# Graph attention and graph convolution on one core: four score tiles in a row from shared PSUM, and both ends reordered

## The chip, the core and the metric

The kernel runs on one core of one Trainium2 chip. A core has a tensor engine (PE, with its weight loads shown as PEld), VectorE (DVE), ScalarE (ACT), GpSimd (POOL) and SyncE (SP), which here only starts DMAs. Each engine works through its own instructions in order. The time is the device time of one execution in microseconds (us); a kernel's time is the median of its runs.

## The reference

There are 32 batches of 512 nodes with 512 features, all in float32, and one adjacency matrix of 512 x 512 for all of them.

```python
# layer 0: attention with 8 heads of 64, masked by the adjacency matrix
q, k, v = x @ Wq + bq, x @ Wk + bk, x @ Wv + bv
weights = softmax(q k^T / 8 + where(adj == 0, -1e9, 0))
x = layernorm(x + weights v)
# layer 1: graph convolution with a normalised adjacency matrix
deg = adj.sum(axis=1)
norm_adj = adj * rsqrt(deg)[:, None] * rsqrt(deg)[None, :]
x = layernorm(x + norm_adj @ (x @ W1) + b1)
```

## The kernel before

**Products.** The products with Wv, Wk, Wq and W1 are made of 512 x 512 matrices cut in two both ways, with seven products of halves instead of eight (`seven`, `second`). Each such *piece* is eight matmuls into one PSUM bank named `mm`, and VectorE or ScalarE adds it to what it belongs to. The seven products need sums and differences of the operands: slots 4, 5, 6 and a changed slot 2 of `XT` (x transposed, made by `combine`), of `wv`, `wk`, `wq`, `w1` (made by `weigh_part`), and of `zT` (made by the `combine` in `convolve`).

**Attention.** A *block* is one batch and one pair of heads, so there are 4 blocks to a batch and 128 in all; the loop over k goes through them. For a block, `scores` makes four score tiles of 128 x 1024 (two heads beside each other), in two calls with two tiles each. Each tile is four matmuls of 64 rows into two PSUM banks. VectorE cuts the tile off at 60 and subtracts the mask (`e<-sc,maskT`), which frees the PSUM, and ScalarE takes the exponent in place. `values` multiplies the tiles by v into one bank, `av`, with 64 columns for each head; VectorE turns that into `yb`, and DMAs bring it to its place in `YT`. GpSimd adds up the tiles for the softmax's sums (`accumulate`, some of it put off through `pending`), and VectorE folds the sums (`fold`, a transpose and a reduction).

**Order.** Every engine's order is the order in which the program is written (`InOrder` pins it). Step k of the loop runs the first two score tiles of block k, folds the sums of block k - 1, runs the values of block k - 1, then the last two score tiles of block k, then a *share* of other work: the values, keys and queries of the next batch and the convolution of the batch before, which is 8 pieces to a block. The lists `main`, `side` and `beside` say which small step follows which piece, and `cut` makes the shares. In the first batch a share has 4 pieces. The convolution's steps are `norm` (layer norm and its float32r part `hi`), `low` (the remainder `lo`), `lift` (adds b1), `grow` (scales by the root of the degree), `first` or `block` (times the adjacency), `second` (times W1), `measure`, `root` and `store`.

**PSUM.** There are eight banks. Three are for pieces and small things (`ps_mm`), two times two for score tiles (`ps_sc`), and one for `av` (`ps_av`).

**Ends.** Ahead of the loop stand the loading and weighing of the weights (`weigh(wv)`, `weigh(wk)` on GpSimd), `turn_first` (x of batch 0 turned by PE), the values and keys of batch 0 and the masks (`adjacency`). `compare` checks that the float32r adjacency lost nothing, and `degrees` makes the powers of the degrees. Behind the loop stands what is left of the last two batches, and `judge` and a count, from which the program decides on the device whether its shortcuts held; if they did not, `general` computes everything again.

Of the kernel before, what the change touches and what calls it, by code (L numbers as in the profile page):

```python
# [9 lines left out]
F32 = mybir.dt.float32  # L10
# [7 lines left out]
P = 128  # L18
H = 8
# [30 lines left out]
def unshifted(  # L50
# [29 lines left out]
    B, N, D = x.shape  # L80
# [9 lines left out]
    small = ctx.enter_context(tc.tile_pool(name="small", bufs=3))  # L90
    ps_mm = ctx.enter_context(tc.tile_pool(name="ps_mm", bufs=3, space=bass.MemoryType.PSUM))
    ps_sc = ctx.enter_context(tc.tile_pool(name="ps_sc", bufs=2, space=bass.MemoryType.PSUM))
    ps_av = ctx.enter_context(tc.tile_pool(name="ps_av", bufs=1, space=bass.MemoryType.PSUM))

# [23 lines left out]
    def turn(b, j):  # L118
# [4 lines left out]
        if j == 0 and b > 1:  # L123
            load_x(b, 1)

    def turn_first(j, i):

        p = ps_mm.tile([P, 2, HALF], F32, name="mm")
        for n in range(2):
            for u in range(2):  # L130
                for q in range(4):
                    at = q * P + (2 * i + u) * 32
                    tensor.matmul(
                        p[32 * q : 32 * (q + 1), u, ts(n, P)], R[0][2 * j + n][:, at : at + 32], ident,
                        start=True, stop=True,
                    )
        (scalar.copy if i else vector.tensor_copy)(XT[:, 2 * j + i], p)

# [102 lines left out]
    def adjacency(m):  # L241


        p = ps_mm.tile([P, N], F32, name="mm")
# [41 lines left out]
    def seven(multiply, first, middle, out):  # L286
# [3 lines left out]
        def piece(k, i, j):  # L290
            p = ps_mm.tile([P, 2, HALF], F32, name="mm")
            multiply(p, i, j)
# [22 lines left out]
    def values_of(b):  # L315


        def multiply(p, i, j):
            for r in range(2):
                for u in range(2):  # L320
                    tensor.matmul(
                        p[:, r, :], XT[:, j, u, ts(r, P)], wv[:, i, u, :],
                        start=u == 0, stop=u == 1,
                    )

        def first(e1, p):
# [46 lines left out]
    def scores(s):  # L373
# [3 lines left out]
        for l in range(2):  # L377
            j = 2 * jj + l
            e = E[s][l]
            p = ps_sc.tile([P, 2, N], F32, name="sc")  # L380
            for k in range(2):
# [26 lines left out]
    def values(s):  # L408
# [3 lines left out]
        if jj == 0:  # L412
            AV[b, g] = ps_av.tile([P, N], F32, name="av")
        av = AV[b, g]
# [45 lines left out]
    def sums(b, c):  # L460


        p = ps_mm.tile([P, N], F32, name="mm")
        for q in range(4):
# [33 lines left out]
    def finish(b):  # L498
# [4 lines left out]
        def inverse_all():  # L503

            p = ps_mm.tile([P, H, NT, 4], F32, name="mm")
            tensor.matmul(
# [11 lines left out]
        def inverse(cs):  # L518
            sT = SM[b]
            p = ps_mm.tile([P, NT, 2, 2, 32], F32, name="mm")  # L520
            for i in range(NT):
# [25 lines left out]
        def turn_values(g):  # L547

            t["y"] = ps_mm.tile([P, NT, P], F32, name="mm")
            for i in range(NT):  # L550
# [46 lines left out]
        def lift(i):  # L597
            gpsimd.tensor_add(YT[b][:, i, :], YT[b][:, i, :], b1_r)

# [31 lines left out]
    def convolve(b):  # L631
# [5 lines left out]
        def first(d):  # L637
            p = ps_mm.tile([P, N], F32, name="mm")
            for m in range(NT):
# [4 lines left out]
        def block(m):  # L644
            if m == 0:
                t["p"] = [ps_sc.tile([P, 2, N], F32, name="sc") for _ in range(2)]
            for part, start, stop in ((HI[b][:, m, :], m == 0, False), (LO[b][m], False, m == NT - 1)):
# [27 lines left out]
        def second(k, i, j):  # L675
            p = ps_mm.tile([P, 2, HALF], F32, name="mm")
            for r in range(2):
# [123 lines left out]
    weigh(wv, gpsimd)  # L801
    weigh(wk, gpsimd)
    first = values_of(0)
# [20 lines left out]
    run(one)  # L824
    shares, rest, within = [], [], []
    for k in range(S + 1):
        b, at = divmod(k, G)
        if at == 1:
# [10 lines left out]
            if b == 0:  # L839
# [3 lines left out]
                beside = {  # L843
                    2: put_off, 3: [(0, degrees, ())] + put_off, 6: put_off, 7: w1_parts[:1] + put_off,
                    8: w1_parts[1:2], 9: turn0 + w1_parts[2:3], 10: put_off + exact[:2], 11: put_off + w1_parts[3:],
                    12: exact[2:], 13: turn1,
                }
                side = early[5:6] + put_off + early[6:] + put_off
                side += sum(([piece] + beside.get(i, []) for i, piece in enumerate(main)), [])
                shares = cut(side, (4, 4, 4, 4))  # L850
            elif b < B - 1:
# [4 lines left out]
                beside = {  # L856
                    0: rest[:1], 1: rest[1:3], 3: rest[3:4] + put_off, 4: rest[4:5],
                    5: rest[5:6] + f["inverse"] + put_off, 6: rest[6:] + f["scale"][:2], 7: f["scale"][2:] + f["add"],
                    8: measure[:2] + put_off, 9: measure[2:], 10: f["root"] + put_off, 11: norm[:1],
                    12: norm[1:2] + low[:1], 13: norm[2:3] + low[1:2], 14: norm[3:] + low[2:3],  # L860
                    15: low[3:] + f["lift"], 16: put_off + grow[:2], 17: put_off + grow[2:], 18: turn0 + f["judge"],
                }
                side = sum(([piece] + beside.get(i, []) for i, piece in enumerate(main)), [])
                side += c["first"] + c["parts"] + kq[5:] + turn1[:1]
                s = c["second"]
                if b < B - 2:
                    side += put_off + s[:1] + put_off + s[1:3] + turn1[1:2] + s[3:4] + turn1[2:3] + s[4:5]
                    side += turn1[3:4] + s[5:6] + c["measure"][:1] + turn1[4:] + s[6:] + c["measure"][1:2]
                    rest = c["measure"][2:] + c["root"] + c["store"]
                    shares = cut(side, (8, 8, 8, 8))  # L870
# [22 lines left out]
        if k < S:  # L893
            scores((*blocks[k], 0))
        if k == 0:
            run(two)
            early = values_of(1)
            run(early[:2])
        if k and blocks[k - 1][0] < B - 1:
            fold(*blocks[k - 1])  # L900
        if k:
            values((*blocks[k - 1], 0))
# [3 lines left out]
            if k == S - 2:  # L906
                sums(blocks[k - 1][0], (k - 1) % G // 2)
        if k == S - 2:
# [12 lines left out]
        if k == 0:  # L921
            run(early[2:3] + put_off + early[3:4] + put_off + early[4:5])
        elif shares:
            run(shares.pop(0))
# [4 lines left out]
    run(sum((pairs[3][i : i + 1] + end["measure"][i : i + 1] for i in (0, 1)), []) + end["halves"][:1] + s[3:5])  # L929
    run(sum((pairs[3][i : i + 1] + end["measure"][i : i + 1] for i in (2, 3)), []) + extend[:1] + end["halves"][1:])  # L930
# [15 lines left out]

    run(e["unload"] + e["parts"] + s[6:] + end["grow"] + extend[2:] + c["measure"][:2])
    s, tail, halves = e["second"], c["measure"][2:] + c["root"] + c["store"], e["halves"]
    run(s[:2] + halves[0] + s[2:3] + tail[:1] + s[3:4] + tail[1:3] + s[4:5])
    p = ps_mm.tile([1, 1], F32, name="mm")  # L950
    tensor.matmul(p, count, ones, start=True, stop=True)
    vector.tensor_scalar(bad, p, -1.0, float(P * B * NT * H + N), op0=ALU.mult, op1=ALU.add)
    run(tail[3:] + s[6:] + e["measure"][2:] + e["roots"][1:] + e["stores"][2:] + s[5:6] + halves[1] + e["roots"][:1])
    run(e["stores"][:2])
# [283 lines left out]
```

## Time and profile before

| what | us |
|---|---|
| median of three runs | 2820.21 (2820.18 to 2822.76) |
| the profiled execution, its own time | 2821.64 |
| its span, first to last instruction | 2819.7 |
| PE busy | 2792.0 |
| VectorE busy | 2177.5 |
| GpSimd busy | 1786.4 |
| ScalarE busy | 1050.1 |

The span is one profiled execution. An engine is busy while one of its instructions runs, and matmuls overlap their neighbours, so a busy PE can still lose time between matmuls of different shapes. Every instruction that goes through `InOrder` is recorded with line 44, so rows are told apart by the names of what they write and read: `sc<-kq` are scores, `av<-e,v` are values, `mm<-...` are pieces. A row `a, b <- c` ends with what the engine waited for before it. A stretch's row gives its length, the busy time of PE, PEld, DVE, ACT and POOL with the number of instructions, the granted PE clock, the DMA engines' share and GB/s. The granted clock was 0.997 over the span.

### The profile page before, as it was taken

How to read it: one execution, taken by the hardware profiler on the slowest of the kernel's cores; microseconds unless marked ns; L12 is line 12 of the kernel's file. 1: busy time of each engine (PE TensorE's matmuls, PEld its weight loads, DVE VectorE, ACT ScalarE, POOL GpSimd, SP SyncE). 2: the span in 40 equal slices, each digit the busy share in tenths (PEclk: the TensorE clock that was granted, in tenths of full speed). 3: DMA queues.
4: the chain of work that ended last, by engine and by line, in shares of the span. 5: the costliest groups of instructions: out<-in, count | busy, mean ns of one | idle time of the engine just before them, and what ended most of it. 6: DMA issues, size and time to landing. Idle time of an engine off the chain costs nothing.

```text
span 2819.7 us, 34592 instructions
## 1 busy us (share of the span) xinstructions
PE 2792.0 (99%) x12540; PEld 1874.8 (66%) x12540; DVE 2177.5 (77%) x3201; ACT 1050.1 (37%) x1323; POOL 1786.4 (63%) x1174
## 2 busy tenths in 40 slices
PE   8999999999999999999999999999999999999997
PEld 6566666666666666666666666666666666666655
DVE  5877877788777787777787778877777777778777
ACT  2333333343333433334333334333343333443343
POOL 3666665666666666666666666666666666666656
PEclk9999999999999999999999999999999999999999
DMA  4111121112221122221112211222112122112211
GB/s 120 32 29 49 49 59 43 43 48 52 57 57 42 38 52 54 57 45 42 49 49 60 53 42 37 53 56 57 42 41 53 49 56 46 42 49 49 60 38 50
DMA packets 379107, 141.04 MB, mean 50 GB/s; under 512 B 277808, under 2 KB 345392, under 8 KB 378928
## 3 DMA queue, kind: packets, MB, share of 16 engines
q1 hardware_dynamic: 377776, 137.17, 20.4%
q8 instruction: 101, 1.65, 0.2%
q10 hardware_dynamic: 1152, 1.57, 0.2%
q14 instruction: 78, 0.64, 0.1%
HBM read 71.83 MB, written 33.55 MB: 37 GB/s over the span
## 4 chain that ended last, share of the span: by engine, by line
PE 97%; DVE 2%; POOL 0%; issue 0%; DMA 0%; ACT 0%; POOLq 0%; DVEq 0%; ACTq 0%
PE mm L44 64%; PE sc L44 17%; PE av L44 16%; DVE e L44 1%; DVE xT L44 0%; DVE plainT L44 0%; POOL xT L44 0%; POOL acc L44 0%; DVE st L44 0%; DVE y L44 0%; DMA xr<-in_x_dram 0%; DVE lo L44 0%; DVE kq L44 0%; DVE lost L44 0%; DVE ve L44 0%
## 5 line engine op out<-in xcount | busy, mean ns | idle before, releaser
L44 ACT ACTIVATE e<-e 128x1024 f32<-128x1024 f32 x512 | 540.9, 1057 | 1075.8 <-DVE e L44 1059.2
L44 POOL TENSOR_TENSOR acc<-acc,e 128x1024 f32<-128x1024 f32 x248 | 587.5, 2369 | 94.3 <-ACT e L44 87.1
L44 DVE SCALAR_TENSOR_TENSOR e<-sc,maskT 128x1024 f32<-128x1024 f32 x512 | 597.9, 1208 | 22.1 <-PE sc L44 21.9
L44 PE MATMUL sc<-kq 64*128 64x512 f32 x2048 | 510.1, 616 | 3.6 <-DVE e L44 3.5
L44 PE MATMUL mm<-xT,wk 128*128 128x256 f32 x1792 | 469.7, 384 | 2.4 <-issue 2.0
L44 PE MATMUL av<-e,v 128*64 128x512 f32 x2048 | 467.9, 598 | 0.0
L44 PE MATMUL mm<-xT,wq 128*128 128x256 f32 x1792 | 459.9, 379 | 0.0
L44 PEld LDWEIGHTS mm<-xT,wk 128*128 128x128 f32 x1792 | 332.2, 190 | 115.9 <-issue 72.9
L44 PE MATMUL mm<-wv,xT 128*128 128x256 f32 x1792 | 405.3, 383 | 1.8 <-DVE xT L44 1.3
L44 PEld LDWEIGHTS mm<-wv,xT 128*128 128x128 f32 x1792 | 336.3, 191 | 72.7 <-issue 25.3
L44 POOL TENSOR_TENSOR acc<-e 128x1024 f32<-128x1024 f32 x126 | 297.2, 2359 | 134.3 <-ACT e L44 134.3
L44 PEld LDWEIGHTS mm<-xT,wq 128*128 128x128 f32 x1792 | 340.5, 190 | 46.3
L44 PEld LDWEIGHTS sc<-kq 64*128 64x128 f32 x2048 | 175.9, 186 | 271.4 <-issue 203.1
L44 PEld LDWEIGHTS av<-e,v 128*64 128x64 f32 x2048 | 135.5, 136 | 316.2 <-issue 293.4
L44 POOL TENSOR_TENSOR yT<-yT,b_r 128x512 f32<-128x512 f32 x124 | 154.6, 1279 | 167.7 <-DVE lo L44 167.7
L44 DVE TENSOR_TENSOR kq<-u,mm 128x512 f32<-128x512 f32 x128 | 88.0, 688 | 221.9 <-PE mm L44 221.6
L44 PE MATMUL mm<-w,zT 128*128 128x256 f32 x992 | 224.9, 379 | 0.7 <-ACT side L44 0.7
L44 POOL TENSOR_TENSOR rstd<-ve,minus_half 128x4 f32<-128x4 f32 (+1 forms) x66 | 66.1, 1001 | 234.1 <-DVE nmu L44 234.1
L44 PEld LDWEIGHTS mm<-w,zT 128*128 128x128 f32 x992 | 188.2, 190 | 28.1 <-issue 1.5
L44 PE MATMUL mm<-adjT,hi 128*128 128x512 f32 x496 | 202.1, 407 | 0.0
L44 POOL TENSOR_TENSOR yT<-yT,xr 128x512 f32<-128x512 f32 x124 | 154.4, 1278 | 73.6 <-DVE yT L44 73.6
L44 PE MATMUL mm<-adjT,lo 128*128 128x512 f32 x496 | 195.9, 395 | 0.5 <-DVE lo L44 0.5
(141 smaller groups left out, 3254.5 us busy)
## 6 DMA issues: line engine op xcount, KB each, us to landing
out_dram<-y SPq DMA_DIRECT2D x127, 256.0 KB, 2.1
x<-in_x_dram SPq DMA_DIRECT2D x248, 128.0 KB, 2.9
yT<-yb SPq DMA_DIRECT2D x496, 64.0 KB, 2.5
xr<-in_x_dram SPq DMA_DIRECT2D x122, 256.0 KB, 3.3
wk<-in_L_gnn_Wk_dram SPq DMA_DIRECT2D x8, 128.0 KB, 5.0
wq<-in_L_gnn_Wq_dram SPq DMA_DIRECT2D x8, 128.0 KB, 4.3
yT<-in_adj_dram SPq DMA_DIRECT2D x1, 1024.0 KB, 6.0
w<-in_L_gnn_weight_dram SPq DMA_DIRECT2D x2, 512.0 KB, 7.6
```

Source lines behind the costliest of these rows:

```text
L44: return self.tc.keep_in_program_order(op(*args, **kwargs))
```

## The change

The change takes one PSUM pool with two-bank buffers, three of them, for both score tiles and pieces (`WIDE`), and a one-bank buffer (`narrow`) that takes every fourth piece; `av` keeps its bank. In the loop, the last two score tiles of block k now come directly behind the fold, ahead of the values of block k - 1, for all but the last three blocks and block 0, where pieces of the next batch lie between. Small steps on VectorE are put behind other pieces than before, so that other ones are the last in a share. In the fill, the differences of batch 0's `XT` are taken from PSUM, `weigh(wk)` is written later, and the bias is added to u2 by VectorE for batches 0 and 1. The comparisons are spread over blocks 1, 2, 4 and 5, the turn of batch 2's second half goes into block 5. In the tail, `norm` of tile 0 goes ahead of a piece, the lifts go behind all the lows (two of them on VectorE), and `judge` and the count go in between the last pieces.

```diff
-    ps_mm = ctx.enter_context(tc.tile_pool(name="ps_mm", bufs=3, space=bass.MemoryType.PSUM))
-    ps_sc = ctx.enter_context(tc.tile_pool(name="ps_sc", bufs=2, space=bass.MemoryType.PSUM))
-    ps_av = ctx.enter_context(tc.tile_pool(name="ps_av", bufs=1, space=bass.MemoryType.PSUM))
+    psum = ctx.enter_context(tc.tile_pool(name="psum", bufs=1, space=bass.MemoryType.PSUM))
+    WIDE = dict(tag="wide", bufs=3)
+    turn_of = {"n": 0, "order": (WIDE, WIDE, WIDE, dict(tag="narrow"))}
+
+    def bank(shape, tags=None):
+        if tags is None:
+            order = turn_of["order"]
+            tags = order[turn_of["n"] % len(order)]
+            turn_of["n"] += 1
+        return psum.tile(shape, F32, name="mm", **tags)
...
     def turn_first(j, i):
...
-        (scalar.copy if i else vector.tensor_copy)(XT[:, 2 * j + i], p)
+        if j == 0:
+            (scalar.copy if i else vector.tensor_copy)(XT[:, i], p)
+        elif i == 0:
+            turned["B12"] = p
+            vector.tensor_sub(XT[:, 4], p, XT[:, 0])
+        else:
+            scalar.copy(XT[:, 3], p)
+            vector.tensor_sub(XT[:, 5], p, XT[:, 4])
+            vector.tensor_sub(XT[:, 6], XT[:, 3], turned["B12"])
...
         def middle(u2, u1, p):
             vector.tensor_add(u2, u1, p)
-            gpsimd.tensor_add(u2, u2, bv_r[:, None, HALF:].to_broadcast([P, 2, HALF]))
+            engine = gpsimd if b > 1 else vector
+            engine.tensor_add(u2, u2, bv_r[:, None, HALF:].to_broadcast([P, 2, HALF]))
...
         def lift(i):
-            gpsimd.tensor_add(YT[b][:, i, :], YT[b][:, i, :], b1_r)
+            engine = vector if b == B - 1 and i < 2 else gpsimd
+            engine.tensor_add(YT[b][:, i, :], YT[b][:, i, :], b1_r)
...
     weigh(wv, gpsimd)
-    weigh(wk, gpsimd)
...
-    combine(0, 0)
-    combine(0, 1)
     run(first[1:2])
-    combine(0, 2)
     combine(0, 3)
     scalar.activation(wq[:, :4], wq[:, :4], AF.Copy, scale=SCALE)
-    run(first[2:])
+    run(first[2:4])
+    weigh(wk, gpsimd)
+    run(first[4:])
...
                 beside = {
-                    2: put_off, 3: [(0, degrees, ())] + put_off, 6: put_off, 7: w1_parts[:1] + put_off,
-                    8: w1_parts[1:2], 9: turn0 + w1_parts[2:3], 10: put_off + exact[:2], 11: put_off + w1_parts[3:],
-                    12: exact[2:], 13: turn1,
+                    0: exact[:1], 2: put_off, 3: put_off + exact[1:2], 6: put_off + [(0, degrees, ())],
+                    7: w1_parts[:1] + put_off, 8: w1_parts[1:2], 9: w1_parts[2:3], 10: put_off + turn0,
+                    11: put_off + w1_parts[3:], 12: exact[2:3],
                 }
+                inner, rest = turn1, exact[3:]
...
                 beside = {
-                    0: rest[:1], 1: rest[1:3], 3: rest[3:4] + put_off, 4: rest[4:5],
-                    5: rest[5:6] + f["inverse"] + put_off, 6: rest[6:] + f["scale"][:2], 7: f["scale"][2:] + f["add"],
-                    8: measure[:2] + put_off, 9: measure[2:], 10: f["root"] + put_off, 11: norm[:1],
-                    12: norm[1:2] + low[:1], 13: norm[2:3] + low[1:2], 14: norm[3:] + low[2:3],
-                    15: low[3:] + f["lift"], 16: put_off + grow[:2], 17: put_off + grow[2:], 18: turn0 + f["judge"],
+                    0: rest[:1] + put_off, 1: put_off + rest[1:3], 2: rest[3:4], 3: rest[4:5] + f["inverse"],
+                    4: rest[5:6] + f["scale"][:2], 5: rest[6:7] + f["scale"][2:] + f["add"], 6: rest[7:],
+                    8: measure[:2] + put_off, 9: measure[2:] + f["root"] + put_off, 10: norm[:1], 11: norm[1:2],
+                    12: norm[2:3] + low[:1], 13: low[1:2], 14: norm[3:] + low[2:3], 16: low[3:] + put_off,
+                    17: put_off, 18: f["lift"] + turn0 + f["judge"],
                 }
                 side = sum(([piece] + beside.get(i, []) for i, piece in enumerate(main)), [])
-                side += c["first"] + c["parts"] + kq[5:] + turn1[:1]
+                side += c["first"] + c["parts"] + grow + kq[5:] + turn1[:1]
...
         if k < S:
             scores((*blocks[k], 0))
+        else:
+            turn_of["n"], turn_of["order"] = 0, (WIDE, dict(tag="narrow"), dict(tag="av"))
...
+        elif at == 1 and b:
+            run(inner)
+            inner = []
         if k and blocks[k - 1][0] < B - 1:
             fold(*blocks[k - 1])
+        if k < S - 3:
+            scores((*blocks[k], 1))
+            turn_of["n"] = 0
         if k:
             values((*blocks[k - 1], 0))
...
-        if k == S - 2:
-            run(within)
-            scores((*blocks[k], 1))
...
-            accumulate((*blocks[k], 0))
-            scores((*blocks[k], 1))
...
-    run(s[5:6] + norm[:2] + low[:1] + block[:1] + low[1:2] + block[1:2] + lift[:1] + extend[1:2] + norm[2:] + low[2:3])
-    run(block[2:3] + low[3:] + lift[1:2] + block[3:] + lift[2:] + end["judge"])
+    run(norm[:1] + s[5:6] + low[:1] + norm[1:2] + block[:1] + low[1:2] + block[1:2] + norm[2:] + low[2:3])
+    run(block[2:3] + low[3:] + block[3:] + lift[3:] + lift[:3] + extend[1:2] + extend[:1])
+    run(e["unload"] + e["parts"] + s[6:] + end["grow"] + extend[2:] + c["measure"][:2])
+    s, tail, halves = e["second"], c["measure"][2:] + c["root"] + c["store"], e["halves"]
+    run(s[:2] + halves[0] + s[2:3] + end["judge"])
```

More of the change, by code (lines that the diff above doesn't have):

```diff
@@ L124, in turn @@
             load_x(b, 1)
+    turned = {}
     def turn_first(j, i):
-        p = ps_mm.tile([P, 2, HALF], F32, name="mm")
+        p = bank([P, 2, HALF])
         for n in range(2):
@@ L241, in adjacency @@
     def adjacency(m):
-        p = ps_mm.tile([P, N], F32, name="mm")
+        p = bank([P, N])
         for n in range(NT):
@@ L290, in piece @@
         def piece(k, i, j):
-            p = ps_mm.tile([P, 2, HALF], F32, name="mm")
+            p = bank([P, 2, HALF])
             multiply(p, i, j)
@@ L379, in scores @@
             e = E[s][l]
-            p = ps_sc.tile([P, 2, N], F32, name="sc")
+            p = psum.tile([P, 2, N], F32, name="sc", **WIDE)
             for k in range(2):
@@ L412, in values @@
         if jj == 0:
-            AV[b, g] = ps_av.tile([P, N], F32, name="av")
+            AV[b, g] = psum.tile([P, N], F32, name="av")
         av = AV[b, g]
@@ L460, in sums @@
     def sums(b, c):
-        p = ps_mm.tile([P, N], F32, name="mm")
+        p = bank([P, N])
         for q in range(4):
@@ L503, in inverse_all @@
         def inverse_all():
-            p = ps_mm.tile([P, H, NT, 4], F32, name="mm")
+            p = bank([P, H, NT, 4], dict(tag="av"))
             tensor.matmul(
@@ L519, in inverse @@
             sT = SM[b]
-            p = ps_mm.tile([P, NT, 2, 2, 32], F32, name="mm")
+            p = bank([P, NT, 2, 2, 32])
             for i in range(NT):
@@ L547, in turn_values @@
         def turn_values(g):
-            t["y"] = ps_mm.tile([P, NT, P], F32, name="mm")
+            t["y"] = bank([P, NT, P], WIDE)
             for i in range(NT):
@@ L637, in first @@
         def first(d):
-            p = ps_mm.tile([P, N], F32, name="mm")
+            p = bank([P, N])
             for m in range(NT):
@@ L645, in block @@
             if m == 0:
-                t["p"] = [ps_sc.tile([P, 2, N], F32, name="sc") for _ in range(2)]
+                t["p"] = [psum.tile([P, 2, N], F32, name="sc", **WIDE) for _ in range(2)]
             for part, start, stop in ((HI[b][:, m, :], m == 0, False), (LO[b][m], False, m == NT - 1)):
@@ L675, in second @@
         def second(k, i, j):
-            p = ps_mm.tile([P, 2, HALF], F32, name="mm")
+            p = bank([P, 2, HALF])
             for r in range(2):
@@ L824, in unshifted @@
     run(one)
-    shares, rest, within = [], [], []
+    shares, rest, within, inner = [], [], [], []
     for k in range(S + 1):
@@ L867, in unshifted @@
                     side += put_off + s[:1] + put_off + s[1:3] + turn1[1:2] + s[3:4] + turn1[2:3] + s[4:5]
-                    side += turn1[3:4] + s[5:6] + c["measure"][:1] + turn1[4:] + s[6:] + c["measure"][1:2]
-                    rest = c["measure"][2:] + c["root"] + c["store"]
+                    side += turn1[3:4] + s[5:6] + c["measure"][:1] + turn1[4:] + s[6:]
+                    rest = c["measure"][1:] + c["root"] + c["store"]
                     shares = cut(side, (8, 8, 8, 8))
@@ L907, in unshifted @@
                 sums(blocks[k - 1][0], (k - 1) % G // 2)
+                run(within)
+        if k < S and k != S - 2:
+            accumulate((*blocks[k], 0))
+        if S - 3 <= k < S:
+            scores((*blocks[k], 1))
+            turn_of["n"] = 0
         if k == S - 2:
-            run(within)
-            scores((*blocks[k], 1))
             pending += [((*blocks[k], jj),) for jj in range(2)]
         elif k < S:
-            accumulate((*blocks[k], 0))
-            scores((*blocks[k], 1))
             if b == B - 1:
@@ L921, in unshifted @@
         if k == 0:
-            run(early[2:3] + put_off + early[3:4] + put_off + early[4:5])
+            run(early[2:4] + put_off + put_off + early[4:5])
         elif shares:
@@ L929, in unshifted @@
     run(sum((pairs[3][i : i + 1] + end["measure"][i : i + 1] for i in (0, 1)), []) + end["halves"][:1] + s[3:5])
-    run(sum((pairs[3][i : i + 1] + end["measure"][i : i + 1] for i in (2, 3)), []) + extend[:1] + end["halves"][1:])
-    run(s[5:6] + norm[:2] + low[:1] + block[:1] + low[1:2] + block[1:2] + lift[:1] + extend[1:2] + norm[2:] + low[2:3])
-    run(block[2:3] + low[3:] + lift[1:2] + block[3:] + lift[2:] + end["judge"])
+    run(sum((pairs[3][i : i + 1] + end["measure"][i : i + 1] for i in (2, 3)), []) + end["halves"][1:])
+    run(norm[:1] + s[5:6] + low[:1] + norm[1:2] + block[:1] + low[1:2] + block[1:2] + norm[2:] + low[2:3])
[3 more added lines that the diff above has]
+    run(s[:2] + halves[0] + s[2:3] + end["judge"])
     count = small.tile([P, 1], F32, name="count")
@@ L945, in unshifted @@
     vector.memset(ones, 1.0)
[L947 to L950, printed above, removed]
+    run(s[3:4] + tail[:1] + s[4:5] + tail[1:3] + s[6:])
+    p = bank([1, 1])
     tensor.matmul(p, count, ones, start=True, stop=True)
     vector.tensor_scalar(bad, p, -1.0, float(P * B * NT * H + N), op0=ALU.mult, op1=ALU.add)
-    run(tail[3:] + s[6:] + e["measure"][2:] + e["roots"][1:] + e["stores"][2:] + s[5:6] + halves[1] + e["roots"][:1])
+    run(tail[3:] + e["measure"][2:] + e["roots"][1:] + e["stores"][2:] + s[5:6] + halves[1] + e["roots"][:1])
     run(e["stores"][:2])
```

## The prediction

> **What bounds the kernel.** I read the page first, then busy time by stretch, then the tensor engine's timeline, then the other engines at both ends.
>
> ```profile
> span 2819.7 us, 34592 instructions
> PE 2792.0 (99%) x12540; PEld 1874.8 (66%) x12540; DVE 2177.5 (77%) x3201; ACT 1050.1 (37%) x1323; POOL 1786.4 (63%) x1174
> PE 97%; DVE 2%; POOL 0%; issue 0%; DMA 0%; ACT 0%; POOLq 0%; DVEq 0%; ACTq 0%
> ```
>
> ```profile
> 0.00:137.00 137.00, 124.79 (x656) 83.37 (x656) 96.45 (x120) 35.27 (x42) 66.93 (x52) 1.00 0.34 77
> 1177.00:2043.00 866.00, 866.00 (x3862) 582.82 (x3860) 670.85 (x981) 326.07 (x410) 555.97 (x361) 1.00 0.20 49
> 2720.00:2820.00 100.00, 84.22 (x377) 52.12 (x375) 81.93 (x164) 41.63 (x57) 62.41 (x52) 0.94 0.15 41
> ```
>
> The first number after a stretch's length is PE's busy time. In the middle PE never rests; all its idle time lies in the first 137 us and the last 100. So the middle gets shorter only if the same matmuls run denser, and the next view shows where they are not dense (start, length, engine, operation, count; a float32 matmul shows as two instructions):
>
> ```profile
> 1406.68 1.02 PE L44 MATMUL mm<-xT,wk 128*128 128x256 f32 x4
> 1407.54 1.03 PE L44 MATMUL mm<-xT,wq 128*128 128x256 f32 x4
> 1408.50 1.99 PE L44 MATMUL sc<-kq 64*128 64x512 f32 x8
> ...
> 1409.03 0.60 PE L44 MATMUL sc<-kq 64*128 64x512 f32 x2
> 1409.46 0.60 PE L44 MATMUL sc<-kq 64*128 64x512 f32 x2
> 1409.89 0.60 PE L44 MATMUL sc<-kq 64*128 64x512 f32 x2
> 1410.41 3.65 PE L44 MATMUL av<-e,v 128*64 128x512 f32 x16
> 1414.00 1.99 PE L44 MATMUL sc<-kq 64*128 64x512 f32 x8
> 1415.91 1.13 PE L44 MATMUL mm<-xT,wk 128*128 128x256 f32 x4
> 1416.88 1.03 PE L44 MATMUL mm<-xT,wq 128*128 128x256 f32 x4
> ```
>
> Full-array matmuls start 0.216 us apart (0.86 for four), score pairs 0.43 apart. At each change of shape time is lost: the last mm before scores takes 0.10 more (0.96 for four), the first score pair 0.53 and the last 0.52 instead of 0.43, and the first mm after scores 0.10 more (0.97). The av run takes 3.59 where eight pairs at 0.43 are 3.43: 0.06 at its entry, 0.10 at its exit. A block now goes mm, sc, av, sc, mm: four changes, about 0.2 us each.
>
> **The middle.** The change runs four score tiles in a row: mm, sc, av, mm. This is so in 124 blocks (k = 1 to 124; k = 0 has mm between its halves, and the last three keep the old order). Removed: av to sc (exit 0.10, entry 0.10) and sc to mm (exit 0.10, entry 0.10). Added: av to mm, which the trace doesn't show. Its exit is av's 0.10. Its entry is bounded below by a transpose after av (0.165 instead of 0.109, so 0.06) and above by twice the mm entry after scores (0.20), which is nearer in kind; I take that entry itself, 0.10. Net 0.40 - 0.20 = 0.20 a block, **25 us** for 124 (bounds 0.10 to 0.24, so 12 to 30). The Trainium skill (TensorEngine Tiling, Key Properties) says that a change of tiling mode drains the engine, and TensorE: Matmul & The Clock Gate (step-by-step, DRAIN) gives a drain as about 128 cycles, 53 ns at its 2.4 GHz. By that alone a change saved is worth 124 x 0.053 = 6.6 us; the row shows 0.2[...], and the row decides.
>
> **What could give it back.** Score tiles and mm pieces now share three two-bank buffers (plus one one-bank buffer for every fourth piece). The fourth score tile needs the first one's buffer. From the start of a block: the first tile is done at 1.1, VectorE starts it at 1.17 (1408.50 to 1409.67 below) and takes 1.2, so it is free at 2.4, 2.5 with the 0.06 to 0.14 that PE needs to follow. The fourth tile's turn comes at 0.53 + 5 x 0.43 = 2.68. Slack 0.2 us, if VectorE's queue is empty by 1.35.
>
> ```profile
> 1408.60 0.69 DVE L44 TENSOR_TENSOR kq<-u,mm 128x512 f32<-128x512 f32 x1 [6.23 <-PE mm L44]
> 1409.67 2.36 DVE L44 SCALAR_TENSOR_TENSOR e<-sc,maskT 128x1024 f32<-128x1024 f32 x2 [0.38 <-PE sc L44]
> 1430.03 1.28 DVE L44 TENSOR_TENSOR y<-y,mm 128x512 f32<-128x512 f32 x2
> 1450.67 3.05 DVE L44 TENSOR_TENSOR yT<-yT,inv 128x512 f32<-128x512 f32 x4
> ```
>
> Now it often isn't: the four yT products end at 1453.64, 2.0 after their block began at 1451.68. The diff moves them, the measures and lo between earlier pieces. I walked VectorE's new order through the four kinds of block with its present durations. Behind the block's start stand: values block, the last v, till 0.6; keys block, one kq, till 0.8; convolution block, one kq, 0.8; second block, the two y of its last piece (1430.03 begins 0.10 after its block), till 1.4, so the first tile is free at 2.5 to 2.65. None reaches 2.68. Within the block VectorE does two tiles, the two fold operations (1.2 each), two tiles, yb: free at 8.8, when pieces start at 7.2. Pieces 1, 2 and 3 take the buffers of tiles 2, 3 and 4, free at 3.5, 7.0 and 8.2, against starts at 7.2, 9.0 and 10.8. The third tile's exponent also needs an old e tile, read by av until 4.7; VectorE comes to it at 5.8. So 0 for the middle; with the cover gone, each 0.1 us late costs 12 us. Behind a late VectorE stand ScalarE's exponents, but av uses them only a block later. POOL has the same adds (2.4 each) in another order; its bias add to u, for which v on VectorE waits, ends about 16.6, and v's piece is done at 16.4. Lift moves behind the adds and grow behind the zT copies; the y that need them come a block later. DMA issues keep their number and their place by piece.
>
> **The ends.**
>
> ```profile
> 26.96 1.10 PE L44 MATMUL mm<-xT,wk 128*128 128x256 f32 x4 [2.02 <-issue]
> 24.28 1.26 POOL L44 TENSOR_TENSOR u<-u,bv_r 128x512 f32<-128x512 f32 x1
> 134.52 2.82 PE L44 MATMUL sc<-kq 64*128 64x512 f32 x8 [3.26 <-DVE e L44]
> 2784.33 1.67 PE L44 MATMUL sc<-adjT,hi 128*128 128x512 f32 x4 [2.19 <-ACT hi L44]
> ```
>
> *Fill.* PE starts keys at 26.96, because its buffer is that of the fifth values piece, which waits for v, v for u, and u's add stands on POOL behind four wk products (until 24.3). The add goes to VectorE. The first XT differences are now taken from PSUM (0.7 each instead of separate 1.45 operations), so XT5 is there at 13.7 and the third values piece starts once POOL has made wv5, about 15.0 (now 16.07). Five pieces end at 23.7. The first keys piece needs scaled wq (ScalarE, 22.54 + 1.91) for its second half, so the second keys piece starts at 25.5 instead of 28.8: **3.3 us**. A fourth buffer removes 0.3 at 51.7. The Trainium skill (SBUF, Who interferes with whom) says that a VectorE operation with two SBUF inputs is blocked by a GpSimd one that reads SBUF. That speaks against the moved add: 0.7 alone, and the two-SBUF differences at 12.82 took 1.55 each beside POOL. With 1.5, v comes at 20.8, when its matmul ends (20.2): nothing lost by either price.
>
> *First batch.* At 53 to 82 PE waits for POOL's u again, which goes to VectorE: 0.4. At k = 5 PE waits 3.26 behind four compares and a turn, and the rows around it stretch by 1.9 more: 5.2 lost. The compares are spread over four blocks and the turn goes behind two score tiles. In exchange k = 5 now has turn and compare in itself, and its last v ends about 2.1 into the next block: 0.75 lost, with 0.2 at k = 4. Net **4.2 us**.
>
> *Tail.* Before 2784.33 PE waits 2.19 for hi: ScalarE's norm of tile 0 stands behind a copy of a piece that is done at 2782.2. It is moved ahead, so hi comes at 2782.1. The lifts go behind the lows, so POOL no longer slows VectorE's norms (1.5 to 0.7). The block of 32 matmuls ends some 2.5 us earlier; the judge's nine small operations (1.5 us) then stand in VectorE's queue near the end, most of it in time that the two moved lifts leave. I take **2.5 us** (bounds 0 to 4).
>
> **Sum.** 25 + 3.3 + 0.3 + 0.4 + 4.2 + 2.5 = 35.7 us, from the profiled execution's 2821.6: 2785.9. Its time is 1.4 above the median (2820.2), so the median of the changed kernel is **2784.5**.
>
> **Rivals.**
> - *VectorE is late by 0.1 to 0.2 us in most blocks.* For: slack is only 0.2, and 0.05 in the second block. Against: the walk above. 124 x 0.15 = 19 back: about 2803.
> - *The shared buffers cost more than the change saves: slower.* One place, the fourth score tile. Each block would have to lose 35.7 / 124 = 0.29 us; one more 0.7 us operation ahead of the first tile in each block costs about 0.5, 62 in all: 2846. For: VectorE's queue is strict and 77% full. Against: the order shows no such operation.
> - *The gap isn't saved:* av to mm costs 0.4, as much as the two changes that it replaces. Only the ends gain, 10.7: about 2810. For: this change occurs nowhere in the trace. Against: every entry and exit that the trace does show is 0.05 to 0.10.
> - *The ends give nothing,* because the next producer is just as late: 2795.
>
> **How the numbers follow.** Likeliest case 0.70 (own range 2777 to 2794), ends nothing 0.05, late by a little 0.13, gap not saved 0.07, slower 0.05. The range reaches from 2776 (av to mm at its low bound, tail at its high) to 2803, which takes in the first rival's middle and leaves out less than 2 in 10. 0.2% (5.6 us) is about what a measurement of this kernel can tell from no change; all cases but the slower one, and a sliver of the late one, lie below that: faster 0.94, same 0.02, slower 0.04.
>
> **What would show it.** Right: sc runs of 16 rows lasting 3.63, av to mm of about 0.2, batches 85.8 long instead of 86.6, PE with no wait for VectorE in the middle; keys at about 25; no 3.26 at k = 5; the hi wait near 0. Wrong: a gap in front of the seventh score pair, a first mm after av that takes over 0.4, batches of 86 or more.

## The result, and the profile after

| | before | after |
|---|---|---|
| median, us | 2820.99 (2820.18 to 2822.76, 4 runs) | 2785.18 (2784.81 to 2786.06, 4 runs) |
| profiled execution, own time | 2821.64 | 2786.06 |
| its span | 2819.7 | 2784.3 |
| PE busy | 2792.0 | 2760.3 |
| VectorE busy | 2177.5 | 2229.2 |

The changed kernel takes 0.9871 of the time before, with an interval of 0.9858 to 0.9884. The forecast was 2784.5, so the total came out as predicted. Several of its terms did not, with opposite signs. Rows of the page of the changed kernel:

```profile
span 2784.3 us, 34624 instructions
...
PE 2760.3 (99%) x12540; PEld 1877.7 (67%) x12540; DVE 2229.2 (80%) x3204; ACT 1049.8 (38%) x1323; POOL 1794.1 (64%) x1170
```

The number of PE instructions is the same, 12540. The changed kernel does the same matmuls in 35.4 us less of span. The same stretches of it as before (length, then busy time of PE, PEld, VectorE, ScalarE and GpSimd, granted PE clock, DMA share, GB/s):

```profile
1177.00:2043.00 866.00, 866.00 (x3903) 590.52 (x3900) 697.24 (x994) 328.74 (x413) 565.10 (x363) 1.00 0.21 50
...
0.00:131.00 131.00, 123.75 (x664) 84.67 (x665) 96.75 (x121) 35.86 (x43) 64.81 (x51) 1.00 0.36 81
2690.00:2790.00 100.00, 77.90 (x358) 48.43 (x354) 74.85 (x156) 41.48 (x57) 58.91 (x49) 0.95 0.15 41
```

In the middle PE is busy all the time before and after, so its busy time says nothing. What changed is the number of matmul instructions that start in the same 866 us: 3903 where there were 3862. The tensor engine's timeline, from the start to the end, answers to the rows shown of before:

```profile
15.73 8.90 PE L44 MATMUL mm<-wv,xT 128*128 128x256 f32 x40 [1.52 <-POOL wv L44]
24.46 1.03 PE L44 MATMUL mm<-xT,wk 128*128 128x256 f32 x4
25.50 1.13 PE L44 MATMUL mm<-xT,wq 128*128 128x256 f32 x4
...
96.05 1.13 PE L44 MATMUL sc<-kq 64*128 64x512 f32 x4 [0.23 <-DVE e L44]
...
145.86 2.26 PE L44 MATMUL sc<-kq 64*128 64x512 f32 x8 [0.30 <-DVE v L44]
...
1430.00 3.70 PE L44 MATMUL sc<-kq 64*128 64x512 f32 x16
1433.63 3.65 PE L44 MATMUL av<-e,v 128*64 128x512 f32 x16
1437.22 1.13 PE L44 MATMUL mm<-xT,wk 128*128 128x256 f32 x4
1438.19 1.03 PE L44 MATMUL mm<-xT,wq 128*128 128x256 f32 x4
...
2747.45 1.19 PE L44 MATMUL sc<-adjT,hi 128*128 128x512 f32 x4 [1.10 <-ACT hi L44]
2749.06 1.19 PE L44 MATMUL sc<-adjT,lo 128*128 128x512 f32 x4 [0.42 <-DVE lo L44]
...
2769.43 1.99 PE L44 MATMUL mm<-w,xT 128*128 128x256 f32 x8 [1.08 <-DVE y L44]
```

- Middle: scores are one row of 16 instructions that lasts 3.63 (1430.00 to 1433.63). The change from `av` to `mm` costs what was taken for it: `av` lasts 3.59, with 0.10 at its exit as before, and the first four `mm` behind it take 0.97 instead of 0.86. There is no wait there.
- Fill: the wait of 2.02 before the keys is gone. Ahead of the 40 values matmuls PE waited 1.25 for VectorE's `xT` before, and now waits 1.52 for GpSimd's `wv`.
- First batch: the wait of 3.26 at block 5 is gone. Two small ones are new, at block 3 and at block 6.
- Tail: of the wait of 2.19 for `hi` 1.10 is left, 0.42 for `lo` is new, and a wait of 1.08 stands before the last eight matmuls.

Where the 35.4 us of span came from, by the first score matmul of some blocks. The second column divides the forecast's terms in the same way (0.2 for each block of the row of four):

| stretch | predicted | measured | how measured |
|---|---|---|---|
| start to k = 0 | 3.6 | 2.90 | 53.67 to 50.77 |
| k = 0 to k = 7 | 4.6 + 6 x 0.2 = 5.8 | 5.57 | 174.12 - 53.67 against 165.65 - 50.77 |
| k = 7 to k = 125 | 118 x 0.2 = 23.6 | 26.29 | 2722.24 - 174.12 against 2687.48 - 165.65 |
| k = 125 to the end | 2.5 | 0.64 | the rest of 35.4 |

### The profile page after: what moved, and what is told of

It is laid out like the page before. It is cut to its first block, busy times and chain, and to the rows that moved or that the text cites. A ratio compares the mean times of both kernels' runs of the same rounds, so it can differ in the third digit from the quotient of the medians.

```text
span 2784.3 us, 34624 instructions
## 1 busy us (share of the span) xinstructions
PE 2760.3 (99%) x12540; PEld 1877.7 (67%) x12540; DVE 2229.2 (80%) x3204; ACT 1049.8 (38%) x1323; POOL 1794.1 (64%) x1170
## 5 line engine op out<-in xcount | busy, mean ns | idle before, releaser
L44 POOL TENSOR_TENSOR acc<-acc,e 128x1024 f32<-128x1024 f32 x248 | 596.9, 2407 | 155.4 <-ACT e L44 147.9
L44 PE MATMUL sc<-kq 64*128 64x512 f32 x2048 | 476.3, 603 | 0.5 <-DVE v L44 0.3
L44 PEld LDWEIGHTS sc<-kq 64*128 64x128 f32 x2048 | 183.7, 186 | 229.1 <-issue 142.4
L44 DVE TENSOR_TENSOR e<-e,mm 128x512 f32<-128x512 f32 x224 | 151.3, 675 | 48.7 <-PE mm L44 48.6
L44 POOL TENSOR_TENSOR xT<-xT 128x512 f32<-128x512 f32 x126 | 159.3, 1276 | 38.5 <-DVE xT L44 31.8
```

The source lines that it names most:

```text
L44: return self.tc.keep_in_program_order(op(*args, **kwargs))
```

## The experiments

Times without an interval are single executions.

**e1: the row of four alone undone.** The changed kernel with the last two score tiles put back behind the values of the block before; everything else of the change stays.

```diff
-        if k < S - 3:
-            scores((*blocks[k], 1))
-            turn_of["n"] = 0
         if k:
             values((*blocks[k - 1], 0))
...
-        if S - 3 <= k < S:
+        if k < S:
             scores((*blocks[k], 1))
             turn_of["n"] = 0
```

> Changed kernel (2785.2 us), one part undone: the last two score tiles of every block come behind the values of the block before again. Shared PSUM, queue order and both ends stay as changed. Theory (one change of matmul shape fewer per block is what the middle gains): 124 blocks lose 0.20 to 0.22 us each, so 25 to 27 us more, 2810 to 2812; the sc run shows as two runs of 8 rows again. Rival (the middle gained because VectorE's queue is clear in front of the scores): nothing is lost, 2785 to 2788.

Measured: 2808.99 (2808.18 to 2809.07, 4 runs), 0.9955 of before (0.9938 to 0.9971), which is 23.8 above the changed kernel. That is 1 below the theory's 2810. A block of e1 on the tensor engine's timeline:

```profile
1419.38 1.99 PE L44 MATMUL sc<-kq 64*128 64x512 f32 x8
1421.30 3.65 PE L44 MATMUL av<-e,v 128*64 128x512 f32 x16
1424.88 1.99 PE L44 MATMUL sc<-kq 64*128 64x512 f32 x8
1426.80 7.17 PE L44 MATMUL mm<-wv,xT 128*128 128x256 f32 x32
```

From the first score to the first piece are 7.42 us, and 7.22 in the changed kernel (1430.00 to 1437.22). A batch of four blocks lasts 86.493 in e1 and 85.707 in the changed kernel: 0.197 a block, 24.4 for 124. So the row of four is worth what the forecast's sum said, and the shared buffers take nothing back. e1's batch is still 0.10 shorter than before's 86.60; that is a different gain, told below.

**e2: the row of four without the new order of VectorE.** The kernel before, with only the shared PSUM and the row of four:

```diff
-    ps_mm = ctx.enter_context(tc.tile_pool(name="ps_mm", bufs=3, space=bass.MemoryType.PSUM))
-    ps_sc = ctx.enter_context(tc.tile_pool(name="ps_sc", bufs=2, space=bass.MemoryType.PSUM))
+    psum = ctx.enter_context(tc.tile_pool(name="psum", bufs=1, space=bass.MemoryType.PSUM))
+    WIDE = dict(tag="wide", bufs=3)
...
+        if k < S - 3:
+            scores((*blocks[k], 1))
+            turn_of["n"] = 0
         if k:
             values((*blocks[k - 1], 0))
```

> Kernel before (2820.2 us) with two parts of the change alone: the shared PSUM and the four score tiles in a row. VectorE's order and both ends stay as before. Theory (VectorE must be free 1.35 us behind a block's start, or the fourth tile waits for the first one's buffer): the trace of before shows its last work ending 2.0 (values block), 2.3 (keys), 0.8 (convolution) and 2.1 us (second) behind the start, so 0.6 + 0.9 + 0 + 0.8 = 2.3 us are lost to a batch against 0.9 gained; 30 batches x 1.4 = 43 us slower than before, about 2863. Rival (a late VectorE is absorbed, the row of four alone gives the gain): 2795.

Measured: 2873.72, so slower than before by 53. Its tensor engine's timeline at a block that follows second products, and then at the two next ones:

```profile
1459.51 2.85 PE L44 MATMUL sc<-kq 64*128 64x512 f32 x12
1462.89 1.13 PE L44 MATMUL sc<-kq 64*128 64x512 f32 x4 [0.53 <-DVE e L44]
...
1485.07 1.13 PE L44 MATMUL sc<-kq 64*128 64x512 f32 x4 [0.46 <-DVE e L44]
...
1507.20 1.13 PE L44 MATMUL sc<-kq 64*128 64x512 f32 x4 [0.63 <-DVE e L44]
```

VectorE at the first of these blocks, in the same kernel:

```profile
1459.61 1.29 DVE L44 TENSOR_TENSOR y<-y,mm 128x512 f32<-128x512 f32 x2
1460.82 0.69 DVE L44 BATCH_NORM_STATS2 st<-y 128x6 f32<-128x512 f32 x1
1461.54 0.18 DVE L44 BATCH_NORM_AGGREGATE mv<-st 128x2 f32<-128x6 f32 x1
1461.64 2.32 DVE L44 SCALAR_TENSOR_TENSOR e<-sc,maskT 128x1024 f32<-128x1024 f32 x2
```

The statistics behind the two y operations keep VectorE from the first score tile until 2.13 after the block's start, the tile's buffer is free about 1.2 later, and the fourth tile starts at 3.38 instead of 2.68. In three of four kinds of block VectorE's queue reaches 2.1 to 2.3 us behind the start. A batch lasts 88.13, 2.43 more than in the changed kernel; 2.3 had been reckoned. The time is about 10 us above the reckoning, and most of that lies in the first blocks: block 1 lasts 19.02 where it took 14.92 before, and block 5 29.78 where it took 27.00. In both, the clock adds to VectorE's lateness: the granted clock stands at 0.50 from 72.52 to 75.93 and from 137.37 to 144.20. The row of four is thus a loss without the new order, and the same row is a gain once VectorE's queue is short at its start.

**e3: the slack measured.** The changed kernel with one more VectorE operation of 0.69 us ahead of each block's first tile, for blocks 5 to 124. Nobody reads its output, and nothing is left out.

```diff
+        if G < k < S - 3:
+            vector.bn_stats(small.tile([P, 6], F32, name="st"), bv_r)
         if k < S:
             scores((*blocks[k], 0))
```

> Changed kernel (2785.2 us) with one more VectorE operation, a bn_stats over 128x512 that nobody reads (0.6 us in its queue), in front of the first score tile of blocks 5 to 124. Theory (slack of about 0.2 us on the fourth tile, as the trace of the changed kernel has it: VectorE's last work ends -0.01, 0.87, 0.79 and 1.39 us behind the start in the four kinds of block): about 0 + 0.05 + 0.05 + 0.57 = 0.65 us to a batch, 20 us in all, 2805, nearly all of it in the block that follows the second products. Rival 1 (no slack at all, the operation costs its length everywhere): 120 x 0.6 = 72, 2857. Rival 2 (the buffers never bind): 2785.

Measured: 2806.94. Two blocks of e3 on the tensor engine, one that follows second products, and one that follows values pieces:

```profile
1419.46 2.85 PE L44 MATMUL sc<-kq 64*128 64x512 f32 x12
1422.63 1.13 PE L44 MATMUL sc<-kq 64*128 64x512 f32 x4 [0.33 <-DVE e L44]
...
1441.51 3.70 PE L44 MATMUL sc<-kq 64*128 64x512 f32 x16
```

The first kind has its VectorE tail lengthened from 1.39 to 2.00 and loses 0.59 a batch. The other three reach 0.60, 1.40 and 1.47 and lose 0, 0 and 0.06. So the limit for VectorE's tail is about 1.4 (1.35 by the forecast): below it an operation more costs nothing, and 0.6 beyond it costs 0.59. In the changed kernel one of four kinds of block stands exactly at it.

**f1, g1, g2: which edit of the fill did it.** f1 gives the values' bias add of batches 0 and 1 back to GpSimd; g1 puts GpSimd's products of `wk` back in front; g2 does both.

```diff
-            engine = gpsimd if b > 1 else vector
-            engine.tensor_add(u2, u2, bv_r[:, None, HALF:].to_broadcast([P, 2, HALF]))
+            gpsimd.tensor_add(u2, u2, bv_r[:, None, HALF:].to_broadcast([P, 2, HALF]))
```

```diff
     weigh(wv, gpsimd)
+    weigh(wk, gpsimd)
     first = values_of(0)
...
-    run(first[2:4])
-    weigh(wk, gpsimd)
-    run(first[4:])
+    run(first[2:])
```

> Edit: in the changed kernel the values' second bias add of batches 0 and 1 goes back from VectorE to GpSimd; all else stays. Nothing is left out. Theory (the moved add is most of what the fill and the first batch gained): the first keys piece waits for GpSimd's parts of wk again and starts near 28 us where it was near 25, second keys piece at 28.5 to 29 where it was 26.5, and block k=1 and 2 give back 0.4 to 1 us: 2787 to 2789. Rival (the landing of wq and wk sets the start of the keys, so that the add is hidden where it was): 2785 to 2786, keys at the same time as in the changed kernel.

> Edit: in the changed kernel GpSimd's four products of wk go back in front of the first values pieces; the values' bias add stays on VectorE. Nothing is left out. Theory (either of the two edits of the fill takes the u add out from behind the wk products, so that one alone is enough): the keys start within 1 us of the end of the values pieces, about 23.5 to 24.5 us, and the time is that of the changed kernel, 2784.5 to 2786. Rival (the later place of the wk products is itself the gain): the keys start near 27 and the time is 2787 to 2789.

> Edit: both undone in the changed kernel: the wk products in front, and the values' bias add of batches 0 and 1 on GpSimd behind them. Nothing is left out. Theory (either alone is enough, both undone brings the wait back): GpSimd adds u near 24.3 to 25.5, PE waits about 2 us ahead of the keys, which start near 26 to 27, second keys piece near 28 to 28.8; 2787.5 to 2789. Rival (the fourth buffer of the shared PSUM already frees the keys from that wait): keys at 24 to 25, 2785.5 to 2786.5.

Measured: f1 2785.74 (2785.37 to 2786.25, 4 runs; 0.9874 of before, 0.9857 to 0.989), g1 2785.28, g2 2787.11. The fill of f1 on the tensor engine, where no wait came back:

```profile
14.79 8.90 PE L44 MATMUL mm<-wv,xT 128*128 128x256 f32 x40 [0.22 <-POOL wv L44]
23.53 1.03 PE L44 MATMUL mm<-xT,wk 128*128 128x256 f32 x4
```

The fill of g2 on the tensor engine and on VectorE:

```profile
15.63 8.90 PE L44 MATMUL mm<-wv,xT 128*128 128x256 f32 x40 [1.32 <-POOL wv L44]
24.37 1.03 PE L44 MATMUL mm<-xT,wk 128*128 128x256 f32 x4
...
26.45 1.10 PE L44 MATMUL mm<-xT,wk 128*128 128x256 f32 x4 [0.18 <-DVE e L44]
```

```profile
25.01 0.69 DVE L44 TENSOR_TENSOR v<-u,mm 128x512 f32<-128x512 f32 x1 [4.93 <-POOL u L44]
```

The time from the first values piece of the run of 40 to the first keys piece was 10.89 before (16.07 to 26.96). It is 8.74 in f1, and 8.74 in g2 too, where GpSimd's u is as late as before and VectorE waits 4.93 for it (4.91 before). So it is the fourth PSUM buffer that freed the keys: the first keys piece no longer needs the buffer of the fifth values piece. In g2 the first keys piece starts 0.64 before VectorE first reads the fifth values piece (25.01). The late v shows only in pieces behind that: its first key to k = 0 takes 26.79, and 26.02 in g1, a loss of 0.77; block 1 loses another 0.60 (14.94 instead of 14.34). Either of the two edits removes the 0.77. The add on VectorE alone removes the 0.60, which f1 shows as well (14.95). So f1's theory (keys near 28) did not hold, and its rival had the time; g1's theory had both the keys and the time. For g2 neither expectation held: keys came when the rival said, and the time lay between the two.

**e4: the judge behind the last square roots.** The changed kernel with the judge's and the count's small VectorE operations taken out from between the last pieces and put behind the last roots, and the count's matmul at the very end.

```diff
-    run(s[:2] + halves[0] + s[2:3] + end["judge"])
+    run(s[:2] + halves[0] + s[2:3])
...
+    run(end["judge"])
     count = small.tile([P, 1], F32, name="count")
```

> Changed kernel (2785.2 us) with judge and the count (nine small VectorE operations, 2.8 us in its tail) moved from between the last pieces to behind the last root, where VectorE waits 1.0 us for GpSimd, and the count's matmul to the very end. Theory (they stood in the queue that ends the program and took back most of what the earlier norm gave): the last piece's matmuls no longer wait 1.1 us for VectorE, the last y comes about 2.2 us earlier, about 0.5 is paid at the new place: 1.5 to 2 us faster, 2783 to 2784. Rival (the tail is bound by the matmuls): no change, 2785.

Measured: 2785.12, the time of the changed kernel, as the rival had it, though not because the matmuls bound the tail. The tensor engine's tail in e4, and the granted clock of the stretch 2746 to 2752 in it (columns as above):

```profile
2748.65 1.79 PE L44 MATMUL sc<-adjT,lo 128*128 128x512 f32 x4 [0.40 <-DVE lo L44]
2750.24 1.91 PE L44 MATMUL sc<-adjT,hi 128*128 128x512 f32 x4
...
2756.84 1.89 PE L44 MATMUL mm<-w,parts 128*128 128x256 f32 x8
2758.57 12.25 PE L44 MATMUL mm<-w,xT 128*128 128x256 f32 x56
```

```profile
2746.00:2752.00 6.00, 4.56 (x13) 3.26 (x14) 4.82 (x14) 4.20 (x7) 3.26 (x4) 0.75 0.00 1
```

The last output products now go through without a gap (56 matmuls in 12.25). From `mm<-w,parts` to the end of the span are 26.5, and 28.3 in the changed kernel: 1.8 gained. In this profile the granted clock was 0.75 in that stretch (1.00 in the changed kernel), and the block with the adjacency took 9.79 instead of 8.53 (from the first `hi` to `mm<-w,parts`): 1.26 lost. The moved operations stand behind that stretch, so the edit did not bring the dip about. One execution can't settle what the edit is worth, so p2 has it again, on top of p1.

**p1 and p2: one change of shape less for two blocks.** If each change of shape costs about 0.2 with its exit and entry, then running two blocks' scores and values together and their pieces behind both must give another 0.2 for two blocks. p1 does this for k = 5 to 120, 58 pairs. The shares' order is unchanged.

```diff
+    def opens(k):
+        return 4 < k < S - 7 and k % 2 == 1
...
+        elif opens(k):
+            later += shares.pop(0)
         elif shares:
-            run(shares.pop(0))
+            run(later + shares.pop(0))
+            later = []
```

The turn of `av` of the block before goes behind the first tile of the pair's second block, the fold of the pair's first block behind its values. p2 is p1 with e4's edit.

> Edit: in the changed kernel, for k = 5, 7, ... 119, the share of block k is held back and run behind the second of block k+1, so that TensorE goes scores(k), values(k-1), scores(k+1), values(k), then sixteen pieces. The transposition of the values' bank goes behind the first score tile of the next block, the folding of block k behind the values of block k+1. Nothing is left out. Theory (each change of matmul shape costs about 0.1 us on its last and 0.1 us on its first matmul): six changes in two blocks become five; gone are the exit of a product into scores (0.09) and the entry of a product behind values (0.10), about 0.19 to 0.20 a pair, 58 pairs, 11.4 us: 2773 to 2775, the pair lasting 0.2 us less and no wait of PE for VectorE. Rival (what the changed kernel gained was the cleared queue of VectorE in front of each block, not the changes of shape): eight score tiles inside 15 us fill VectorE's queue, the second row of four scores finds its buffers late by 0.3 to 1 us, and 58 pairs lose more than they gain: 2790 to 2830.

> Edit: the kernel of pairs, and besides the judging of the sums and the count moved behind the last square roots, the count's matmul to the very end. Nothing is left out. Theory: as the pairs, and the 1.08 us in which PE waits for VectorE ahead of the last output products is gone, as it was when the judge alone was moved (mm<-w,xT x56 without a gap there; 1.85 us gained from the second products to the last VectorE op): 2772 to 2774, or 1 us more where the granted clock dips in the conv matmuls of the last batch. Rival (the end is set by the outputs' store and the count's own chain, about 2 us behind the last root): the same time as the pairs or 1 us more.

Measured: p1 2773.32 (2773.08 to 2773.60, 4 runs), 0.9829 of before (0.9813 to 0.9846); p2 2772.26 (2771.68 to 2773.06, 4 runs), 0.9824 (0.9808 to 0.9841). A pair of p1 on the tensor engine:

```profile
1486.87 3.71 PE L44 MATMUL sc<-kq 64*128 64x512 f32 x16
1490.51 3.65 PE L44 MATMUL av<-e,v 128*64 128x512 f32 x16
1494.09 3.70 PE L44 MATMUL sc<-kq 64*128 64x512 f32 x16
1497.72 3.65 PE L44 MATMUL av<-e,v 128*64 128x512 f32 x16
```

Two pairs of a batch last 42.49 and 42.82; the same blocks take 42.69 and 43.03 in the changed kernel. That is 0.20 and 0.21 a pair, and PE waits nowhere in the pair. The price of a change of shape, taken from the trace of before, thus foretold a kernel that had not been run, to within a microsecond (11.4 expected, 2785.18 - 2773.32 = 11.9 measured). p2 is 1.1 below p1. In the two profiled executions the stretch from `mm<-w,parts` to the end is 28.0 in p1 and 26.6 in p2, so the judge's late place gives 1.4 there, although p2's profile, too, has the dip of the clock (9.78 for the block with the adjacency, 8.53 in p1). p2 is the fastest of all these kernels, 12.9 below the changed one.

## Why the prediction was right, and where it wasn't

**The row of four: right, and for its reason.** The forecast took 0.20 a block from exits and entries of the trace of before, and 0.10 for the one change that this trace lacked. e1 puts the row at 0.197 a block, and the rows of after put the new entry at 0.104. The drain of about 128 cycles that the Trainium skill gives (TensorE: Matmul & The Clock Gate, step-by-step, DRAIN), by an estimate 53 ns, would have made 6.6 us of it; e1 and the rows of after show nearly four times that. The weight loads fit the larger price: inside a run before, each load of 0.19 us starts beside the matmul ahead of its own, and at 1414.00 and 1415.91, where the shape changes, the first load starts only with its own matmul. How much of the 0.2 is the load was not tried. The rival that the gap isn't saved has fallen.

**The middle gave 2.7 more than that: a term was missing.** In the kernel before, PE also waited for a buffer once in a batch, which the forecast put at nothing ("In the middle PE never rests"). Its rows on VectorE and PE, and behind the dots the same matmuls of the changed kernel:

```profile
1446.63 0.69 DVE L44 TENSOR_TENSOR v<-u,mm 128x512 f32<-128x512 f32 x1 [1.38 <-POOL u L44]
1447.23 0.68 DVE L44 TENSOR_TENSOR e<-e,mm 128x512 f32<-128x512 f32 x1
1447.81 0.38 PE L44 MATMUL mm<-folded,spread 128*128 128x128 f32 x2
1448.06 1.97 PE L44 MATMUL mm<-wv,xT 128*128 128x256 f32 x8
...
1422.78 0.38 PE L44 MATMUL mm<-folded,spread 128*128 128x128 f32 x2
1423.00 5.35 PE L44 MATMUL mm<-wv,xT 128*128 128x256 f32 x24
```

With three buffers, the values piece behind `mm<-folded,spread` takes that of the fifth values piece, which VectorE reads last in `e<-e,mm`, late because GpSimd's u is late. VectorE ends at 1447.91, and the next piece starts at 1448.06, 0.25 behind the small matmul; in the changed kernel it is 0.22, with another 0.07 saved on the piece's first matmul, 0.10 in all. Three things say that this is a wait for the buffer. The piece's weight load begins 0.12 behind VectorE's end. In e2, where VectorE ends at the same point but there are more buffers, the load does not wait. And once before, in the last batch (2718.47), where VectorE had been done for about a microsecond, the old bank costs nothing. So it is there 30 times, 3.1 us, and PE's busy share doesn't show it, since the matmul ahead is counted as busy through the wait. With it the middle is 24.4 + 3.1 = 27.5, against 25.

**The slack of VectorE: right.** The forecast's walk gave tails of 0.6, 0.8, 0.8 and 1.4 behind the four kinds of block; they are -0.01, 0.87, 0.79 and 1.39. The fourth tile starts at 2.68 in each. e2 shows the slower rival as real (it is what happens without the new order), and e3 shows its threshold. What the forecast put at 0.5 for an operation of 0.7 in each block was too much: it costs that only in the kind of block that is already at the limit, and in place of 62 us it cost 21.8 (2806.94 - 2785.18), of which 30 batches x 0.65 = 19.5 lie in the blocks measured.

**The fill: about the size, by the wrong step.** The step "the add goes to VectorE" was named as what lets the keys start. f1 and g2 show that the shared pool's fourth buffer does it, even with u as late as before; the add is worth 0.6 at block 1 and is one of two ways to another 0.77. It took 1.76 beside GpSimd's product of `wk`, a little over the dearer of the forecast's two prices, and the keys did not wait for it. The other part held: from GpSimd's first product of `wv` to the run of 40 values matmuls are 2.67 instead of 3.63, since `XT` comes from PSUM. In this profile k = 0 came only 2.90 earlier, not 3.6, because the loads landed later: `wv` at 13.06 instead of 12.44, and the scaled `wq`, for which the second half of the first keys piece waits, a microsecond later (ScalarE starts it at 23.54 instead of 22.54). Counted from GpSimd's first product of `wv`, k = 0 stands at 41.23 before, 37.71 after, and 37.43 in f1 and g1: 3.5 to 3.8 gained.

**The first batch: right in sum.** The forecast read 3.26 of wait and rows that "stretch by 1.9 more" at block 5 of before. Most of that stretch is the clock, which stands at 0.50 there from 136.09 to 139.50, by an estimate half of 3.41, 1.7 us; in the changed kernel it does not fall there. Predicted 4.6 with the 0.4 of the first blocks; 5.57 less 6 x 0.2 for the row is 4.4. Block 5 lost nothing (21.45), and block 6 lost 0.85 to the v that ends late, where 0.75 was forecast. The 0.5 that a comparison costs at block 3 (1.93 us on VectorE beside GpSimd) was not in the sum; the 0.2 at block 4 did not come. No run undoes the new places of the comparisons alone; e2, with the old ones, keeps the loss at block 5 (29.78).

**The tail: wrong, 0.6 instead of 2.5.** `hi` came when it was forecast, 26.67 behind the first score of k = 127 (2782.1 is 26.6 behind it), and its matmuls start at 26.73, where they started at 28.84 before. The wait for it was not near 0, though, because PE is there earlier too. The block of 32 matmuls ends 2.69 earlier, by the same count. That this agrees so well with the 2.5 is partly luck: in the profile of before the clock had fallen in that block, in the changed kernel's it had not, and in e4's, where it fell, the block ends only 1.42 earlier. The step that failed is "the judge's nine small operations (1.5 us) then stand in VectorE's queue near the end, most of it in time that the two moved lifts leave". VectorE of before, and behind the dots of the changed kernel:

```profile
2790.84 1.26 DVE L44 TENSOR_SCALAR low<-inv 128x32 f32<-128x32 f32 x1
2792.14 1.23 DVE L44 SCALAR_TENSOR_TENSOR low<-inv,low 128x32 f32<-128x32 f32 x1
...
2764.47 0.57 DVE L44 TENSOR_SCALAR low<-inv 128x32 f32<-128x32 f32 x1
2765.08 1.20 DVE L44 SCALAR_TENSOR_TENSOR low<-inv,low 128x32 f32<-128x32 f32 x1
...
2767.20 0.16 DVE L44 TENSOR_TENSOR count<-count,more 128x1 f32<-128x1 f32 x1
2767.28 0.68 DVE L44 TENSOR_TENSOR u<-e,mm 128x512 f32<-128x512 f32 x1
```

The nine take 2.81 in the changed kernel (2764.47 to 2767.28), and u stands behind them, whose piece PE had finished. The price of 1.5 was a misreading: in the trace of before they already took 3.54 (2790.84 to 2794.38), beside the block with the adjacency, where they held up no matmul. In the changed kernel the first two end within 0.06 of the ends of two of GpSimd's additions (2764.99 and 2766.22); in e4, where GpSimd works only on 128 x 2 tiles, they take 0.17 and 0.19. No run undoes the earlier norm alone, so its part is read from the two traces. The tail gave 2.69 and took back 2.0 (from `mm<-w,parts` to the end 26.2 before, 28.3 after), of which e4 and p2 return 1.8 and 1.4. That the forecast's total held is luck: this miss of 1.9 and the late loads were offset by the 2.7 of the middle, which was not in the sum.

## What to carry to other kernels

Where PE shows as busy all the time, count the changes of matmul shape: here each cost about 0.1 us on the last matmul of the old shape and 0.1 on the first of the new, and fewer, longer runs of one shape paid at that price twice in a row. Such a run needs its consumer's queue to be short at its start, and how short can be computed from the buffers: below the limit one more operation is free, above it each tenth is paid in full. When an edit gains what was forecast, still ask which line gained it, by undoing lines one by one and together, and give small operations at the end the price that the trace shows for them beside the engine that runs there, not their price alone.

## What was not expected of the hardware

After waits of PE the granted clock fell in some executions and not in others. After the wait of 1.1 us for `hi` in the tail it was 1.00 in the changed kernel's profile and in p1's, 0.75 in e4's and 0.83 in p2's, over the stretches of 6 us that hold it. The fall cost 1.26 us in e4. Before, it fell at the same place, behind the wait of 2.19:

```profile
2781.00:2787.00 6.00, 3.81 (x13) 2.79 (x12) 5.73 (x12) 4.28 (x6) 5.76 (x6) 0.82 0.00 0
```

The length of the gap alone doesn't decide it, since it was 1.10 or 1.11 in e4, p2, p1 and the changed kernel. The clock records of these traces show more. A fall goes to 0.50 and lasts 3.41 us or twice that, and it starts a whole number of 3.41 us behind the clock's first rise (e4: 8.11 and 2749.01, 803 times). In the 3.41 us ahead of the fall PE was idle, by the profile's ends of matmuls, for 1.50 in e4 and 1.51 in p2, which hold both the wait for `hi` and that for `lo`; on the same grid it is 1.34 in the changed kernel and 1.44 in p1. So it may be chance, by where the grid lies, that decides. That is not shown: in the fill of before a stretch with 1.92 idle (23.45 to 26.86) was followed by no fall.
